# Layer 0's end in an explicit order, sort positions turned by VectorE, ties by products, and the first table tile in two halves

## The chip, the cores and the metric

The kernel runs on one core of a Trainium2 chip. A core has TensorE (matrix products, called PE in the profile, its weight loads PEld), VectorE (DVE), ScalarE (ACT), GpSimd (POOL), and SyncE (SP), which here only issues transfers. The five engines run their own instruction streams and wait for each other by semaphores. Transfers issued by SP, by ACT and by POOL run on the same 16 DMA engines. The metric is the device time of one launch in microseconds (us).

## The reference, cut to what matters

Four graph layers run one after the other on 2708 nodes of 128 features; each normalises x, applies a relu and adds its result to x. Layers 0 and 1 are the ones that the change touches:

```python
# layer 0: h = relu(layernorm(x)); A = adj, 2708 x 2708
z  = leaky_relu(lap_mul(A, h) @ W1 + b1, 0.1)       # lap_mul: d*(A @ (d*h)), d = 1/sqrt(row sums of A)
d2 = maximum(sq[:, None] + sq[None, :] - 2*(z @ z.T), 0)
S  = exp(-sqrt(d2 + 1e-10) / 2)
S  = where(rank within the row < 4, S, 0)            # only the four nearest nodes of each row stay
x  = x + lap_mul(S + A, h) @ W2 + b2
# layer 1: h = relu(layernorm(x))
XW = h @ W;  s_col = XW @ a[0, :128];  s_row = XW @ a[0, 128:]
den = exp(leaky_relu(s_row[:, None] + s_col[None, :], 0.01))
num = A @ den;  att = where(num != 0, den / num, 0)
x  = x + A @ (att @ XW)
# layer 2: h @ W_self + (A @ h / max(row sums, 1)) @ W_neigh
# layer 3: relu((A @ h) @ kernel + bias)
```

In layer 1, each column of num depends on its node only through s_col, and the leaky relu changes its slope where s_row + s_col changes its sign. If the nodes are sorted by s_row, num for any node lies between two rows of a table of running sums. The kernel builds that table instead of the dense product.

## The kernel before, in words

The 2708 nodes are cut into T = 22 tiles of 128 rows; the last, tile 21, has 20 rows. Columns are cut into six blocks of 512 (the last 148), one PSUM bank each, `acc(0)` to `acc(5)`; tiles go in six groups of four (`GROUPS`, the last one has two). Two more banks, the `ps` tiles of the pool `ps_s`, take short products in turn. The matrix comes in transposed, in row tiles ("chunks", 1354 KB each), through four buffers of the pool `big`; five tiles (17 to 21) can stay in SBUF, in buffers `res17` to `res21`.

**Order.** A scheduler behind the kernel language orders each engine's instructions by priority and readiness. `pin(ins)` ties one instruction behind the one that was written before it on its engine; `tc.issue_after` ties a block behind a given instruction. All else may move. Every engine then runs its stream in order, so that an instruction that waits holds all behind it. `pin` is used on the transfers of SP, on the first product of some groups and on some VectorE operations.

**Degree sums** (L366-405). The chunks are streamed once, TensorE adds up their rows with a matrix of ones (L373), the sums are copied out (L193, L195), turned (L395) and become d. The node features are normalised and multiplied by W1 and W2 beside this (L341, L352).

**First aggregation** (`aggregate(y1, to_z)`, products on L284). For every streamed tile, six products go into the six banks. At the end the resident tiles are added bank by bank, and `done(b)` takes each finished bank on: it becomes z, its transpose and its squared norms.

**Strips** (L510-535). For each tile TensorE makes 128 rows of the distances (L512, L520), ScalarE copies them into a strip of SBUF (L527), VectorE finds the eight largest values (MAX8, L529) and their places (FIND_INDEX8, L531). For tiles from `LATE = T - 4` on, the places are looked for later (`find_last`, L549), so that the degrees of S + A come sooner. Strips 18 and 19 have buffers of their own, all others use `big`.

**Second aggregation and the near terms** (L571-760). y2 is scaled (L577, L579), written to DRAM in two transfers (`ydr`, L583) and aggregated again. POOL gathers the near rows out of ydr, one indirect transfer for each tile and each of the four neighbours (`add_near`, L604, 88 in all, 23 buffers `gath`); VectorE adds each to xs (L610, the "near terms"). `done_l0` takes each bank on: a ScalarE copy (L650), four transposes, the addition to xs (L644), the layer norm (`layernorm_relu`, L211-221). Then come the row terms r of layer 1, for groups 0 to 3 by TensorE (`terms`) and for groups 4 and 5 by a product and a sum on VectorE (`last_terms`, L680-699), and the column terms (L708).

**Counting** (`place`, `places_of`, L808-882). The position of a node in the sorted order is a count of comparisons. For tile t VectorE compares all later nodes' r with the tile's (mask, L844), ScalarE adds up each row of the mask (L845), and TensorE adds up its columns with ones into banks 2 and 3 (L822). Within the tile itself, `own_tiles` (L722-728) makes a comparison in which a tie counts one way. After four tiles, `places_of` copies a row of counts (L858), TensorE turns it into a column by products with a single one (L862), VectorE adds the rest (L874), and POOL scatters the nodes to their places in `order_d` (L879). Between the tiles the totals are made (`total`, L913): the column sums of exp(0.01 r) A, for which 13 chunks are loaded again (L902).

**Table** (L1004-1124). The sorted list is read back and turned; `fetch(t)` (L1015) gathers 126 rows of the matrix in sorted order into `mov`; with the two running rows on top, TensorE multiplies them by `wt` (L1106), VectorE and ScalarE copy the result out (L1110, L1111), and SP stores it in the DRAM table (L1122). Then every node takes its two rows of the table (L1145), and the rest of layer 1 and layers 2 and 3 follow; the change doesn't touch them.

Of the kernel before, what the change touches and what calls it, by code (L numbers as in the profile page):

```python
# [18 lines left out]
P = 128  # L19
# [6 lines left out]
def kernel(  # L26
# [46 lines left out]
    def pin(ins):  # L73

        return tc.keep_in_program_order(ins)

# [99 lines left out]
    one_b = ones_b[:, 0:1]  # L176
# [20 lines left out]
    def acc(b):  # L197
        return ps_a.tile([P, 512], F32, name=f"acc{b}")

# [166 lines left out]
    for i in range(T):  # L366
        c = chunk(i)
        w = width(i)
        if 3 <= i < 3 + 3 * NG:
            weighted((i - 3) // 3, i % 3)  # L370
        for b, (k0, n) in enumerate(KBS):
            g = 32 * (b % 4)
            nc.tensor.matmul(  # L373
                sums[b // 4][g : g + 32, :n],
                ones[:w, :32],
                c[:w, k0 : k0 + n],
                start=(i == 0),
                stop=(i == T - 1),
            )
        if i < FIRST:  # L380
            del resident[i]
    sum_rows = lay.tile([P, 1024], F32, name="sum_rows", tag="U")
# [112 lines left out]
    LATE = T - 4  # L495
# [3 lines left out]
    def strip(t):  # L499
        if LATE <= t < LATE + 2:  # L500
            return lay.tile([P, N], F32, name=f"strip{t}", tag="UZ"[t - LATE])
# [67 lines left out]
    nc.scalar.activation(dinv2, deg2s, AF.Exp, scale=-0.5)  # L569
    y2 = lay.tile([P, T, D], F32, name="y2", tag="Y")  # L570
    ydr = dram.tile([P * T, D], F32, name="ydr")  # L571
    for i in range(2):
        resident[i] = chunk(i)
    for t0, t1 in ((0, T // 2), (T // 2, T)):
# [14 lines left out]
    for t in (T - 2, T - 1, *range(LATE, T - 2)):  # L589
# [10 lines left out]
    def add_near(t, late=False):  # L600
        w = width(t)
        for k in range(TOPK):
            g = res.tile([P, D], F32, name="gath", bufs=23)
            nc.gpsimd.indirect_dma_start(  # L604
                out=g[:w, :],
                out_offset=None,
                in_=ydr[:, :],
                in_offset=bass.IndirectOffsetOnAxis(ap=near_u[:w, t, k : k + 1], axis=0),
            )
            term = nc.vector.scalar_tensor_tensor(  # L610
                xs[:w, t, :],
                g[:w, :],
                simd[:w, t, k : k + 1],
                xs[:w, t, :],
# [3 lines left out]
            if late and k == 0:  # L618
                pin(term)
# [34 lines left out]

# [20 lines left out]
    def last_terms(g):  # L675

        t0, t1 = GROUPS[g]
        k0, n = KBS[g]
        prod = res.tile([P, 4, D], F32, name="prod")
        nc.vector.tensor_tensor(  # L680
# [4 lines left out]
        )  # L685
        e = min(t1, T - 1)
        nc.vector.tensor_reduce(r_nat[:, t0:e], prod[:, : e - t0, :], AX.X, ALU.add)
        if e < t1:
            nc.vector.tensor_reduce(
                r_nat[:TAIL, e:t1], prod[:TAIL, e - t0 : t1 - t0, :], AX.X, ALU.add  # L690
            )
        p = ps_s.tile([P, 512], F32, name="ps")
        for t in range(t0, t1):
            w = width(t)
            o = (t - t0) * P
            nc.tensor.transpose(
                p[:, o : o + w], r_nat[:w, t : t + 1].to_broadcast([w, P]), ident[:w, :w]
            )
        return nc.scalar.copy(row_all[:, k0 : k0 + n], p[:, :n])
# [13 lines left out]
    def own_tiles(g, pool):  # L713
        t0, t1 = GROUPS[g]
        for c0, c1, w in ((t0, min(t1, T - 1), P), (max(t0, T - 1), t1, TAIL)):
            n = c1 - c0
            if n <= 0:
# [3 lines left out]
            eq = pool.tile([P, 4, P], BF16, name="eq", tag="spare")[:w, :n, :w]  # L721
            pin(nc.vector.tensor_tensor(eq, rows_, mine, ALU.is_equal))  # L722
            nc.vector.tensor_tensor(
                eq, eq, tri[:w, None, :w].to_broadcast([w, n, w]), ALU.mult
            )
            o = own[:w, c0:c1, :w]
            nc.vector.tensor_tensor(o, rows_, mine, ALU.is_le)
            nc.vector.tensor_tensor(o, o, eq, ALU.subtract)


    late = {0: (15,), 1: (16,), 2: (17,), 3: (18, 19), 4: ()}

    def done_l0(g, s2):
        to_x1(g, s2)
        if g < NG - 1:
            layernorm_relu(h1, g)
            for t in late[g]:
                add_near(t, late=True)
        if 1 <= g < NG - 1:
            terms(g - 1)  # L740
        if g == NG - 1:
            last_terms(g - 1)
        if g > 2:
# [634 lines left out]
```

## Time and profile before

| what | value |
|---|---|
| three timed runs | 1194.0, 1194.6 and 1188.27 us, median 1194.0 |
| the profiled execution | 1289.18 us, of which the span from first to last instruction 1287.3 |
| PE, PEld, DVE, ACT, POOL busy | 1056.8, 499.3, 561.4, 409.7, 245.7 us |
| mean TensorE clock in that execution | 0.902 of full speed |
| DMA | 298.76 MB, 232 GB/s over the span |

The stages of that execution, from the timeline (us from the span's start):

| stage | from | to |
|---|---|---|
| degree sums | 0 | 93.5 |
| first aggregation | 93.5 | about 204 |
| strips | about 216 | 334.4 |
| second aggregation | 337.3 | 528.9 |
| end of layer 0, to the first comparison of the counting | 528.9 | 552.3 |
| counting and totals | 552.3 | 610.2 |
| table | 610.2 | 785 |
| rest of layer 1 | 785 | 960 |
| layers 2 and 3 | 960 | 1287.3 |

A line of the timeline gives the start, the duration, the engine, the line of the kernel, the operation, its output and inputs, the shape and how many there are; in brackets stands the idle time before it and what ended it. "issue" means that the engine waited for nothing that the profile shows. The clock row gives, in 40 slices of 32 us, the TensorE clock that was granted, in tenths.

### The profile page before, as it was taken

What the parts mean: (1) busy time and instruction counts of PE and PEld (TensorE: products, weight loads), DVE (VectorE), ACT (ScalarE), POOL (GpSimd) and SP (SyncE); (2) the same over time, 40 slices, a digit from 0 to 9 for tenths busy, and PEclk for the clock granted to TensorE, in tenths of its full rate; (3) what the DMA queues carried; (4) which work ended last, traced back from release to release, by engine and by line L of the source; (5) the groups of instructions that cost most, each with busy time, mean ns of one, the idle gap of its engine ahead of it and who ended that gap; (6) DMA issues with size and microseconds to landing.
All of it is one profiled execution on the core that took longest, in us unless ns stands there. A gap on an engine that the chain in (4) does not pass through costs nothing. (4 is left out here: it accounts for less than half of the span.)

```text
span 1287.3 us, 10181 instructions
## 1 busy us (share of the span) xinstructions
PE 1056.8 (82%) x3603; PEld 499.3 (39%) x3603; DVE 561.4 (44%) x1177; ACT 409.7 (32%) x636; POOL 245.7 (19%) x211
## 2 busy tenths in 40 slices
PE   4879999999763379797677771787879999999998
PEld 1324444444221134454333330333334445545444
DVE  2020026999832001783466663899970012104003
ACT  3100014544300000475567644687840012003000
POOL 4000000000277700134211103577500000000000
PEclk9989999999875579788899896698889999999999
DMA  9997800001553361256999997999949945761841
GB/s 344 422 383 276 302 3 1 1 1 43 212 202 96 94 253 50 90 233 245 274 406 395 345 348 269 423 414 419 417 184 395 326 164 181 265 245 54 306 159 43
DMA packets 38800, 298.76 MB, mean 232 GB/s; under 512 B 6735, under 2 KB 9710, under 8 KB 12290
## 3 DMA queue, kind: packets, MB, share of 16 engines
q1 hardware_dynamic: 24798, 203.76, 42.0%
q0 software_dynamic: 13952, 94.36, 19.7%
q8 instruction: 28, 0.46, 0.1%
q14 instruction: 22, 0.18, 0.0%
HBM read 265.76 MB, written 32.87 MB: 232 GB/s over the span
## 5 line engine op out<-in xcount | busy, mean ns | idle before, releaser
L284 PE MATMUL acc<-chunk,y 128*128 128x512 f32 (+1 forms) x408 | 180.3, 591 | 74.7 <-issue 58.4
L1213 PE MATMUL acc<-hi,xw 128*128 128x512 f32 (+3 forms) x264 | 124.2, 634 | 57.8 <-DVE hi L1203 57.8
L1106 PE MATMUL acc<-mov,wt 128*128 128x512 f32 (+1 forms) x264 | 115.4, 592 | 40.7 <-DMA mov<-in_adj_dram,src_u 39.2
L284 PE MATMUL acc<-chunk,h 128*128 128x512 f32 (+1 forms) x384 | 148.3, 542 | 0.0
L604 POOL DMA_INDIRECT gath<-ydr,near_u x88 | 83.8, 952 | 337.5 <-DMA ydr<-y 245.9
L284 PEld LDWEIGHTS acc<-chunk,y 128*128 128x128 f32 x408 | 79.5, 205 | 175.5 <-issue 162.0
L512 PE MATMUL acc<-zT 128*128 128x512 f32 (+2 forms) x264 | 112.7, 559 | 0.4 <-ACT strip L527 0.3
L1213 PEld LDWEIGHTS acc<-hi,xw 128*128 128x128 f32 (+1 forms) x264 | 55.7, 220 | 126.3 <-issue 66.1
L1110 DVE COPY mov<-acc 2x512 f32<-2x512 f32 x126 | 74.3, 611 | 61.1 <-PE acc L1106 60.5
L284 PEld LDWEIGHTS acc<-chunk,h 128*128 128x128 f32 x384 | 68.6, 190 | 73.2 <-issue 73.1
L1106 PEld LDWEIGHTS acc<-mov,wt 128*128 128x128 f32 x264 | 52.1, 205 | 103.8 <-issue 82.3
L527 ACT COPY strip<-acc 128x512 f32<-128x512 f32 (+2 forms) x132 | 60.7, 556 | 61.0 <-issue 35.8
L284 PE MATMUL acc<-chunk,attended 128*128 128x512 f32 x192 | 73.1, 542 | 2.5 <-DMA chunk<-in_adj_dram 2.5
L1145 POOL DMA_INDIRECT lo<-table,lo_u x22 | 58.0, 2638 | 68.6 <-issue 41.1
L1111 ACT COPY knots<-acc 128x512 f32<-128x512 f32 x88 | 50.2, 590 | 62.9 <-DVE mov L1110 56.4
L1195 ACT ACTIVATE hi<-hi,lam 128x2708 f32<-128x2708 f32 (+3 forms) x24 | 56.5, 2363 | 35.6 <-issue 26.7
L1191 DVE SCALAR_TENSOR_TENSOR hi<-lo,lam,hi 128x2708 f32<-128x2708 f32 (+3 forms) x24 | 67.1, 2801 | 1.0
L1203 DVE SCALAR_TENSOR_TENSOR hi<-row_all,inv_s,hi 128x2708 f32<-128x2708 f32 (+3 forms) x24 | 67.0, 2797 | 0.4 <-ACT hi L1196 0.4
L512 PEld LDWEIGHTS acc<-zT 128*128 128x128 f32 (+1 forms) x264 | 45.0, 185 | 51.7 <-issue 41.9
L529 DVE MAX8 top_v<-strip 128x8 f32<-128x2708 f32 (+1 forms) x22 | 64.4, 2967 | 0.4 <-ACT strip L527 0.4
L650 ACT COPY u2T<-acc 128x512 f32<-128x512 f32 (+1 forms) x6 | 3.2, 533 | 168.3 <-PE acc L284 168.2
L1196 ACT ACTIVATE hi<-hi,hb 128x2708 f32<-128x2708 f32 (+3 forms) x24 | 56.5, 2361 | 0.7
(281 smaller groups left out, 1179.5 us busy)
## 6 DMA issues: line engine op xcount, KB each, us to landing
chunk<-in_adj_dram SPq DMA_DIRECT2D x108, 1354.0 KB
table<-knots SPq DMA_DIRECT2D x20, 1354.5 KB
res<-in_adj_dram SPq DMA_DIRECT2D x9, 1354.0 KB
chunkY<-in_adj_dram SPq DMA_DIRECT2D x2, 1354.0 KB
chunkU<-in_adj_dram SPq DMA_DIRECT2D x2, 1354.0 KB
res<-in_adj_dram SPq DMA_DIRECT2D x8, 211.6 KB
ydr<-y SPq DMA_DIRECT2D x2, 704.0 KB
gath<-ydr,near_u POOLq DMA_INDIRECT x88
```

The lines of the kernel that those rows point to most:

```text
L284: nc.tensor.matmul(out[b][:, :n], y[r, i, :], chunk(i)[r, k0 : k0 + n], start=(i == 0), stop=(i == T - 2),)
L512: mm = nc.tensor.matmul(zz[b][:w, :n], zT[:, cols(t)], zT[:, k0 : k0 + n], start=True, stop=False)
L527: copied = nc.scalar.copy(s[:w, k0 : k0 + n], zz[b][:w, :n])
L529: nc.vector.max(top_v[:w, t, :], s[:w, :])
L604: nc.gpsimd.indirect_dma_start(out=g[:w, :], out_offset=None, in_=ydr[:, :], in_offset=bass.IndirectOffsetOnAxis(ap=near_u[:w, t, k : k + ...
L1106: nc.tensor.matmul(p[:, :n], wt[:, t, :], moving[t][:, k0 : k0 + n], start=True, stop=True)
L1110: nc.vector.tensor_copy(moving[t + 1][:2, k0 : k0 + n], p[:2, :n])
L1145: nc.gpsimd.indirect_dma_start(out=dst[:w, :], out_offset=None, in_=table[:, :], in_offset=bass.IndirectOffsetOnAxis(ap=idx[:w, t : t + 1] ...
L1191: nc.vector.scalar_tensor_tensor(num, lo[:w, c], kap, num, op0=ALU.mult, op1=ALU.add)
L1195: nc.scalar.activation(num, num, AF.Ln, scale=sc)
L1203: nc.vector.scalar_tensor_tensor(att[:w, c], row_all[:w, c], inv_s[:w, t : t + 1], att[:w, c], op0=ALU.max, op1=ALU.mult,)
L1213: nc.tensor.matmul(py[b][:, :n], xw[:w, t, :], att[:w, k0 : k0 + n], start=(t == T - 1), stop=(t == T - 2),)
```

## The change

It has six parts; in the diff below lines of "..." mark what is left out.

- An `Ordered` wrapper pins whatever is issued through `pe`, `dve` and `act`. `warm(p, n)` issues n pinned bf16 products of 512 columns whose result isn't used.
- Degree sums: tile 21 is taken before tile 20; three warm products follow each of the last six tiles. 16 more stand before the second aggregation and 14 before the table.
- Strips: `LATE` is T - 5; strips 17, 20 and 21 take the buffers of resident tiles 17, 18 and 19, which the second aggregation loads again (`back=5`). Four chunks instead of two are asked for ahead of the ydr writes, which are three instead of two.
- End of layer 0: the banks of groups 4 and 5 are only collected in `done_l0`; what follows is written out in order. Tile 21's four neighbours are gathered in one transfer of 4 x 32 rows, with indices and weights set in place by eight small transfers on ACT's queue, and added by one product. Group 3's row terms come from VectorE too. The transposes of groups 3 to 5 for the column terms move behind `rmax`, those column terms into `node_terms`.
- Counting: the mask takes in the tile's own columns, `own` holds only the ties on one side of the diagonal and on it, and is subtracted by a product with -1. `places_of` turns the counts by up to four VectorE transposes of 32 rows instead of copy and products. Two totals leave the loop.
- Table: tile 0 is fetched in two halves of its columns and stored in two halves.

```diff
+    class Ordered:
+        def __getattr__(self, name):
+            return lambda *a, **k: pin(getattr(self.engine, name)(*a, **k))
+    pe, dve, act = Ordered(nc.tensor), Ordered(nc.vector), Ordered(nc.scalar)
...
+    def warm(p, n):
+        for _ in range(n):
+            pin(nc.tensor.matmul(p, ident_b, ident_b[:, None, :].to_broadcast([P, 4, P]), start=True, stop=True))
...
-    for i in range(T):
+    for n_, i in enumerate([*range(T - 2), T - 1, T - 2]):
...
+        if n_ >= T - 6:
+            warm(acc(0), 3)
...
-    LATE = T - 4
+    LATE = T - 5
...
-        if LATE <= t < LATE + 2:
-            return lay.tile([P, N], F32, name=f"strip{t}", tag="UZ"[t - LATE])
+        if t in (LATE, T - 2, T - 1):
+            i = T - L0_RES + (LATE, T - 2, T - 1).index(t)
+            del resident[i]
+            return res_rows.tile([P, N + 1], F32, name=f"strip{t}", tag=f"res{i}")[:, :N]
+        if t > LATE:
+            return lay.tile([P, N], F32, name=f"strip{t}", tag="UZ"[t - LATE - 1])
...
+    warm(acc(5), 16)
...
-    for i in range(2):
+    for i in range(4):
         resident[i] = chunk(i)
-    for t0, t1 in ((0, T // 2), (T // 2, T)):
+    for t0, t1 in ((0, 9), (9, 17), (17, T)):
...
-    for t in (T - 2, T - 1, *range(LATE, T - 2)):
+    for t in range(LATE, T):
         find_last(t)
...
+    for k in range(TOPK):
+        for dst, src in ((near_p, near_u), (simd_p, simd)):
+            nc.scalar.dma_start(dst[32 * k : 32 * k + TAIL, :], src[:TAIL, T - 1, k : k + 1])
...
+    def last_near():
+        g = gathered(near_p)
+        dve.tensor_scalar(four_w, four_w, simd_p, None, op0=ALU.mult)
+        p = ps_s.tile([P, 512], F32, name="ps")
+        pe.matmul(p[:TAIL, :P], four_w[:, :TAIL], g, start=True, stop=True)
+        return p
...
-            eq = pool.tile([P, 4, P], BF16, name="eq", tag="spare")[:w, :n, :w]
-            pin(nc.vector.tensor_tensor(eq, rows_, mine, ALU.is_equal))
-            nc.vector.tensor_tensor(eq, eq, tri[:w, None, :w].to_broadcast([w, n, w]), ALU.mult)
             o = own[:w, c0:c1, :w]
-            nc.vector.tensor_tensor(o, rows_, mine, ALU.is_le)
-            nc.vector.tensor_tensor(o, o, eq, ALU.subtract)
+            pin(nc.vector.tensor_tensor(o, rows_, mine, ALU.is_equal))
+            nc.vector.tensor_tensor(o, o, tri[:w, None, :w].to_broadcast([w, n, w]), ALU.mult)
-    late = {0: (15,), 1: (16,), 2: (17,), 3: (18, 19), 4: ()}
+    late = {0: (15,), 1: (16,), 2: (17,), 3: (18,)}
...
     def done_l0(g, s2):
+        if g >= NG - 2:
+            complete.append(s2[g])
+            return
...
+    column_terms(0)
+    add_near(T - 3, dve)
+    x1(E4)
+    for t in range(*GROUPS[E4]):
+        moments(t)
+    roots(E4)
+    x1(E5)
+    normed(E4)
+    p = last_near()
+    prod = row_sums(E4 - 1)
+    natural(E4 - 1, prod)
+    as_row(E4 - 1)
+    column_terms(1)
+    column_terms(2)
+    dve.tensor_tensor(xs[:TAIL, T - 1, :], xs[:TAIL, T - 1, :], p[:TAIL, :P], ALU.add)
+    moments(T - 1)
+    add_near(T - 2, dve)
+    moments(T - 2)
+    roots(E5)
+    prod = row_sums(E4)
+    normed(E5)
+    natural(E4, prod)
+    as_row(E4)
+    natural(E5, row_sums(E5))
+    last_row = as_row(E5)
...
+        for b, (k0, n) in enumerate(KBS):
+            c0, c1 = max(a, k0), k0 + n
+            if c0 < c1:
+                count(c0, c1, ones_b, mk[:w, c0:c1], t == 0, False)
+        count(a, e, minus_b, own[:w, t, :w], False, e == N or e % 512 == 0)
...
-        mine = spare.tile([P, 512], F32, name="mine", bufs=2)
-        nc.vector.tensor_copy(mine[g : g + 1, :n], cnt[b // 4][g : g + 1, :n])
-        for t in range(t0, t1):
...
+        mine = spare.tile([P, 4, 32], F32, name="mine", bufs=2)
+        rows_ = cnt[b // 4][g : g + 32, :].rearrange("p (t f) -> p t f", f=P)
+        for r in range(0, P, 32):
+            m = sum(r < width(t) for t in range(t0, t1))
+            nc.vector.transpose(mine[r : r + 32, :m, :], rows_[:, :m, r : r + 32])
...
-        if 1 <= t <= len(here) + 4 or t in (15, 16, 18, 20):
+        if 1 <= t <= len(here) + 4 or t in (16, 19):
             total(done)
...
+        for c in (slice(0, HALF), slice(HALF, N)) if t == 0 else (slice(0, N),):
+            nc.gpsimd.indirect_dma_start(
+                out=m[2:, c],
...
+                element_offset=c.start,
...
     weights(0)
+    warm(acc(5), 14)
...
-            nc.sync.dma_start(table[t * P + s0 : (t + 1) * P, :], o[s0:, :])
+            for c in (slice(0, HALF), slice(HALF, N + 1)) if t == 0 else (slice(0, N + 1),):
+                nc.sync.dma_start(table[t * P + s0 : (t + 1) * P, c], o[s0:, c])
```

## The prediction

> **What bounds the kernel now.** I read the page first (shares, clock row), then 25-us windows, then the timeline by engine where a slice looks odd, then the waits of the counting stage.
>
> ```profile
> span 1287.3 us, 10181 instructions
> ...
> PE 1056.8 (82%) x3603; PEld 499.3 (39%) x3603; DVE 561.4 (44%) x1177; ACT 409.7 (32%) x636; POOL 245.7 (19%) x211
> ...
> PEclk9989999999875579788899896698889999999999
> ```
>
> TensorE carries the kernel, but its clock sags in slices 12 to 15. The windows (us, busy time with count for PE, PEld, DVE, ACT, POOL, then clock, DMA share, GB/s) show why:
>
> ```profile
> 350.00:375.00 25.00, 20.28 (x52) 9.04 (x51) 9.19 (x31) 0.00 (x0) 18.90 (x21) 0.94 0.66 244
> 375.00:400.00 25.00, 7.88 (x9) 2.54 (x9) 6.89 (x21) 0.00 (x0) 18.90 (x21) 0.50 0.36 107
> 400.00:425.00 25.00, 7.89 (x9) 2.58 (x9) 6.05 (x18) 0.00 (x0) 18.91 (x21) 0.50 0.35 108
> 425.00:450.00 25.00, 8.89 (x9) 2.69 (x10) 0.00 (x0) 0.00 (x0) 17.80 (x19) 0.50 0.34 104
> ```
>
> TensorE does nine matmuls in 25 us and waits for nothing visible, while POOL issues gathers at an undisturbed pace. This execution took 1289.2 us (span 1287.3 and 1.9 around it), the timed runs 1188.3 to 1194.6, median 1194.0: 95.2 less. The same 132 products take 99 us in the undisturbed aggregation (1182.5 to 1281.3). Begun at 337.3, with 1.8 us of half clock, they would end at 438.4, not 528.9: 90.5 us. I therefore take the crawl to belong to the profiled execution; that is an inference.
>
> Without the crawl, who ends layer 0? The timeline has the pieces (start, duration, then idle before and its releaser):
>
> ```profile
> 79.07 1.90 PE L373 MATMUL ps<-res,ones 128*32 128x512 f32 x12 [0.62 <-DMA res<-in_adj_dram]
> ...
> 84.85 5.38 PE L373 MATMUL ps<-res,ones 128*32 128x512 f32 x24 [3.13 <-DMA res<-in_adj_dram]
> ...
> 326.22 2.67 ACT L527 COPY strip<-acc 20x512 f32<-20x512 f32 x6 [2.76 <-issue]
> ...
> 331.40 2.96 DVE L529 MAX8 top_v<-strip 20x8 f32<-20x2708 f32 x1
> ...
> 344.20 1.03 POOL L604 DMA_INDIRECT gath<-ydr,near_u  x1 [245.88 <-DMA ydr<-y]
> ...
> 447.34 0.95 POOL L604 DMA_INDIRECT gath<-ydr,near_u  x1 [0.30 <-issue]
> ...
> 552.28 1.56 DVE L844 TENSOR_SCALAR mask<-row_all,r_nat 128x2580 bf16<-128x2580 f32 x1 [0.78 <-ACT row_all L699]
> ...
> 619.71 7.16 PE L1106 MATMUL acc<-mov,wt 128*128 128x512 f32 x12 [6.53 <-DMA mov<-in_adj_dram,src_u]
> ```
>
> From 344.20 to 447.34 there are 83 gathers, 103.1/82 = 1.26 us each (the last five waited for buffers). All 88 end their issue at 344.2 + 88 x 1.26 = 455.1; a gather is used 3.0 us after its issue starts (the 60th starts near 418.5, its term runs at 421.2), so the last term is near 457. From the last term (547.7) to the first mask (552.28) takes 4.6, so the mask begins near 461. By TensorE: 438.4 plus the profile's 23.4 us from last product to mask gives 461.8. Counting back, 1194.0 less the 1.9 and the 735.0 from mask to end gives 457. So **POOL's gathers and the engines' tail end layer 0 within a few us of each other**, both well behind the last product.
>
> [...] after 3.13 us of idleness 24 sums take 5.38 us where 12 took 1.90, and at 93.5 starts are 0.85 apart, 0.43 after 98.8. [...] the 3.0 above includes 0.95 of issue.
>
> **The change part by part.**
>
> *1. Degree sums.* The 20-row tile 21 goes ahead of tile 20, and three bf16 matmuls follow each of the last six tiles. Behind the last transfer there remain 12 sums at full clock, 1.9, not 24 at half, 5.38: -3.5. The small transfer now goes first: 212 KB at 423 GB/s is 0.5, and if it spreads badly 0.8: +0.65. The next aggregation starts warm: its first 5.3 us of half-speed starts (93.5 to 98.8) take half, -2.7. The final three warm matmuls, [...] lie in the 0.88 us in which TensorE waits for sum_rows. **-5.5** (0 if the clock still drops, to -6.5).
>
> *2. Strips.* From 216.8 VectorE runs without a gap to 334.4: 22 MAX8 and 18 FIND_INDEX8 at 2.9. LATE one lower moves one FIND behind the sums: -2.9, but the last strip is complete only at 328.9, so MAX8 ends at 331.9: **-2.5** (0 to -2.9). The moved search is five times 3.0 instead of four, in front of the near terms only; POOL runs ahead by 23 buffers (29 us). Chunks 2 and 3 are issued by SP ahead of the ydr writes; their buffers come free near 317, so SP isn't held. In exchange three resident tiles are reloaded: 3 x 3.3 = 9.9 us of DMA inside the aggregation; even as a full TensorE stall it ends at 434.1 + 9.9 = 444, before the gathers. The 16 warm matmuls [...] lie between 328.9, when their bank is copied out, and 334.8[...]. They and the warm start end the products 1.8 earlier, which waits for gathers.
>
> *3. Layer 0's end.* Tile 21's four gathers become one with a 0.2-us matmul: 3 x 1.26 = **-3.8** (0 to -7, if the engine order alone was binding). Eight small DMAs on ACT's queue, 0.8 each by SP's three y copies in 2.44 us, 6.5 in all, run near 353; ACT's next work is the first bank, near 420 without the crawl. The pinned VectorE order waits for tile 19's terms (443), with x1, moments and row sums, about 5 us, queued behind; tile 20's terms come at 449.7, so this fits with a us to spare. After the last term prod (0.69) comes before the reciprocal, in a 0.5-us wait: +0.2; ydr in three pieces, -0.3. hT's three transposes and their ACT copies (0.59, 0.59, 0.28) move into the counting stage; they hold the two ps buffers before the totals for about 1 us, covered by VectorE's masks.
>
> *4. Counting.* The waits of 575 to 612 (engine, waited for: us, times, longest):
>
> ```profile
> PE acc L862 <- DVE mine L858: 5.8, 3, 3.5
> DVE to_u L874 <- PE acc L862: 3.4, 3, 1.9
> ```
>
> VectorE loses five copies of 0.68 and one of 0.30 (3.7) and gains 24 transposes of 32 rows by up to 128 columns. The trace has none; nearest are 128 columns from PSUM at 0.29 and 1x512 at 0.68. [...] so I take 0.28: +6.7. Bounds: half of that, +3.4, and twice the 512-column copy, 1.36 each, +32.6. Ties: is_le and subtract go, group 1 moves in: 6.1 to 5.3, -0.8. Masks widen by 128 columns, 0.07 x 22 = +1.5, two extra short ones +0.4. Sum +4.1 of VectorE work; half of it falls in the first 25 us, where VectorE is full: +2. The round trip through TensorE, 3.4, goes. **-1.5** (-5 to +6 short of the dear transpose). Behind a transpose the next masks queue, as behind the copy before. Twelve column-term matmuls (about 0.15 each) move in too, off the path: VectorE doesn't wait for them before tile 16. Two totals leave the loop; the trace already has seven after the last count (598.9 to 610.2), with the turn of the sorted list pinned behind them, so I count nothing; a further total there would cost 1.1 to 1.9.
>
> *5. Table start.* Half a fetch lands first: its data came from about 614 to 619.7, and the first 57% would be there near 617.2; 14 warm matmuls [...] keep the clock, so the first twelve take about 5 instead of 7.2. The store begins near 621.5, not 628; but DMA share is 1.0 from there to 750, so only the mixing with fetches helps: DMA moves 211 to 249 GB/s at 620-630 and over 400 later; 6.5 us x 150 GB/s is 1 MB, 2.4 us. The extra fetch issue is +1.05 on POOL, hidden by queued data. The first tile's store in two costs SP one more issue of 0.33, where SP waits for copies. **-2.0** (0 to -4).
>
> Sum: -5.5 - 2.5 - 3.8 - 1.5 - 2.0 = -15.3. On the profiled execution 1289.2 - 15.3 = 1273.9, if its crawl kept its length; on the median **1178.7, so 1179**.
>
> **Rivals.** *A, the clock stays low and the tail isn't gather-bound.* Parts 1 and 3 give nothing, 4 and 5 half: 1194 - 2.5 - 1.8 = 1189.7. For it: the tie at 461; against: 81.8 to 84.85 is the only long gap there. *B, the halves don't lead*: the first product waits for the whole fetch, and counting, fed by an unbroken 36-us stream of chunks (561 to 597), gives nothing. 1194 - 11.8 = 1182.2. *C, slower: VectorE's transposes.* With price p, and VectorE then the bound of the whole stage, part 4 is 24p - 3.7 - 0.8 + 1.9 - 3.4 = 24p - 6.0. At 1.36 that is +26.6, and 1194 - 13.8 + 26.6 = 1206.8. It decides from 24p - 6.0 = 13.8, at 0.83 us each. Against it: no PSUM operation of 128 columns here takes over 0.35.
>
> **How the numbers follow.** Forecast 0.58, B 0.17, A 0.13, C 0.12. Half a per cent (6 us) is what a measurement tells from no change. Faster 0.75, same 0.13, slower 0.12. The best ends give about 1169; forecast alone 1170 to 1187. To leave out 2 in 10 the range goes to A and stops short of C: 1167 to 1196.
>
> **What the profile would show.** Right: L373's last tile near 1.9; one FIND fewer before the last MAX8; 85 gathers; transposes near 0.28; first L1106 twelve near 5 us, two early stores. Wrong: transposes above 0.6, TensorE waiting for chunks behind the reloads, VectorE idle in the pinned order after its last gather has landed.

## The result and the profile after

| | median | lowest to highest | runs |
|---|---|---|---|
| kernel before | 1192.45 us | 1188.27 to 1196.36 | 20 |
| changed kernel | 1187.68 us | 1184.36 to 1193.61 | 20 |

The ratio is 0.9962, with a 95% interval from 0.9946 to 0.9978: 4.8 us faster by the medians, about a third of the 15.3 forecast. A repetition of the changed kernel gave 0.9972 (0.9952 to 0.9992), 2.8 us by the medians. Ratios are not quotients of the medians; where the two differ much, both are given.

On some of the chips used, every execution of every kernel, timed ones too, shows the crawl of TensorE that the prediction describes and takes about 70 to 90 us more, while on others none does, so figures are compared within one chip's runs unless the text says otherwise. The profile of before that the prediction read has the crawl; the profile after has not.

The page of the changed kernel:

```profile
span 1183.2 us, 10230 instructions
...
PE 1029.7 (87%) x3613; PEld 488.3 (41%) x3613; DVE 561.0 (47%) x1190; ACT 409.0 (35%) x636; POOL 243.6 (21%) x209
...
PEclk9999999999998995989989857899999999999999
```

The row of 5 to 7 in slices 12 to 15 of the clock is gone. Because of that a plain comparison of the two profiles misleads: the crawl stood between them, and so did its after-effects. The timeline of the changed kernel, with the lines that answer to those of the prediction:

```profile
86.51 1.90 PE L396 MATMUL ps<-res,ones 128*32 128x512 f32 x12
...
324.76 2.97 DVE L559 MAX8 top_v<-strip 20x8 f32<-20x2708 f32 x1 [0.29 <-ACT strip L557]
...
330.65 27.53 PE L306 MATMUL acc<-chunk,y 128*128 128x512 f32 x72 [2.26 <-DVE y L610]
361.38 21.43 PE L306 MATMUL acc<-chunk,y 128*128 128x512 f32 x48 [3.20 <-DMA chunk<-in_adj_dram]
386.23 32.04 PE L306 MATMUL acc<-chunk,y 128*128 128x512 f32 x84 [3.41 <-DMA chunk<-in_adj_dram]
...
443.69 0.94 POOL L647 DMA_INDIRECT gath<-ydr,near_u  x1 [0.30 <-DVE xs L699]
446.75 0.87 PE L84 MATMUL ps<-ident,u2T 128*128 128x128 f32 x6 [0.27 <-ACT u2T L84]
...
454.56 1.48 DVE L84 SCALAR_TENSOR_TENSOR xs<-gath,simd,xs 128x128 f32<-128x128 f32 x4
...
460.97 1.63 DVE L982 TENSOR_SCALAR mask<-row_all,r_nat 128x2708 bf16<-128x2708 f32 x1 [1.46 <-ACT row_all L84]
...
521.70 4.71 PE L1245 MATMUL acc<-mov,wt 128*128 128x512 f32 x12
530.94 6.48 PE L1245 MATMUL acc<-mov,wt 128*128 128x512 f32 x12 [3.64 <-DMA mov<-in_adj_dram,src_u]
```

What to see: the degree sums of the last tile run warm (1.90 us). The second aggregation stops twice for a chunk, 3.20 and 3.41 us, after reloads went out on the same queue. The last gather is issued at 443.69, but its term is added only at 454.56, where VectorE's written order puts it: the gathers don't set the end. The first table products start early and at full clock (granted 1.00 from 521.7 to 526.4 us; 0.67 in the profile of before, 619.7 to 626.9), and the second tile then waits 3.64 us for its rows.

The kernel before without the crawl is seen in one of the runs below, which differs from it only in the table stage (`table_only`). Its timeline up to there:

```profile
332.00 79.61 PE L294 MATMUL acc<-chunk,y 128*128 128x512 f32 x204 [9.60 <-DVE y L589]
...
448.25 0.89 POOL L614 DMA_INDIRECT gath<-ydr,near_u  x1 [0.30 <-issue]
448.88 0.67 PE L272 MATMUL ps<-ident,u2T 128*128 128x128 f32 x2
449.59 0.35 DVE L654 SCALAR_TENSOR_TENSOR xs<-ps,dinv,xs 128x128 f32<-128x128 f32 x1 [1.97 <-PE ps L272]
...
453.30 0.69 DVE L690 TENSOR_TENSOR prod<-h,wrow 128x512 f32<-128x512 f32 x1 [1.72 <-ACT h L231]
454.03 0.69 DVE L697 TENSOR_REDUCE r_nat<-prod 128x4 f32<-128x512 f32 x1
454.63 1.76 DVE L620 SCALAR_TENSOR_TENSOR xs<-gath,simd,xs 128x128 f32<-128x128 f32 x5
...
462.41 1.56 DVE L854 TENSOR_SCALAR mask<-row_all,r_nat 128x2580 bf16<-128x2580 f32 x1 [0.78 <-ACT row_all L709]
...
476.32 1.20 POOL L889 DMA_INDIRECT order_d<-pay,to_u  x1 [27.18 <-DVE to_u L884]
...
508.74 0.90 POOL L889 DMA_INDIRECT order_d<-pay,to_u  x1 [0.30 <-issue]
```

Here 204 products run without a gap. The last gather is issued at 448.25, and the trace has its data landed at 450.45. VectorE reaches the last terms only at 454.63. Before them, in its stream, stand the additions of the last bank, which wait for TensorE's transposes (449.59), and then the row terms of group 4, which wait for ScalarE (453.30). TensorE makes the transposes of the last bank at 448.88, 9.9 us after its last product at 439.0: in its stream stand, ahead of them, transposes of group 3, row terms and column terms, three of which wait for ScalarE. In the changed kernel the transposes come at 446.75, 1.1 us after the last product at 445.65. From each profile the length of each stage, in us:

| kernel, one profiled execution each, no crawl | first to second aggregation | products of the second | last product to first mask | mask to first table fetch | fetch to row gathers (L1145; L1285 after) |
|---|---|---|---|---|---|
| table_only (stands for before) | 242.8 | 107.0 | 23.4 | 52.8 | 173.1 |
| changed kernel | 238.6 | 115.0 | 15.3 | 53.5 | 166.1 |
| changed kernel, again | 240.3 | 114.9 | 15.3 | 53.5 | 168.8 |
| reload_only | 244.3 | 115.9 | 23.3 | 53.3 | 171.7 |
| order_count | 243.7 | 108.5 | 15.4 | 53.5 | 168.9 |
| old_strips2 | 241.1 | 108.5 | 16.9 | 52.2 | 168.9 |
| late_reload2 | 238.6 | 111.5 | 15.3 | 53.4 | 169.6 |

Two columns in the middle carry the case: layer 0's end won 8.1 us, and the products ahead of it lost 8.0.

### The profile page after: what moved, and what is told of

It is laid out like the page before. It is cut to its first block, busy times and chain, and to the rows that moved or that the text cites. A ratio compares the mean times of both kernels' runs of the same rounds, so it can differ in the third digit from the quotient of the medians.

```text
span 1183.2 us, 10230 instructions
## 1 busy us (share of the span) xinstructions
PE 1029.7 (87%) x3613; PEld 488.3 (41%) x3613; DVE 561.0 (47%) x1190; ACT 409.0 (35%) x636; POOL 243.6 (21%) x209
## 5 line engine op out<-in xcount | busy, mean ns | idle before, releaser
L1353 PE MATMUL acc<-hi,xw 128*128 128x512 f32 (+3 forms) x264 | 119.0, 610 | 61.2 <-DVE hi L1343 61.2
L306 PE MATMUL acc<-chunk,y 128*128 128x512 f32 (+1 forms) x408 | 158.5, 550 | 10.7 <-DMA chunk<-in_adj_dram 6.6
L1245 PE MATMUL acc<-mov,wt 128*128 128x512 f32 (+1 forms) x264 | 115.0, 589 | 28.4 <-DMA mov<-in_adj_dram,src_u 28.0
L647 POOL DMA_INDIRECT gath<-ydr,near_u x84 | 80.8, 961 | 265.7 <-DMA ydr<-y 240.4
L306 PEld LDWEIGHTS acc<-chunk,y 128*128 128x128 f32 x408 | 74.5, 193 | 94.9 <-issue 88.4
L1353 PEld LDWEIGHTS acc<-hi,xw 128*128 128x128 f32 (+1 forms) x264 | 53.5, 211 | 126.7 <-DVE hi L1343 64.3
L1245 PEld LDWEIGHTS acc<-mov,wt 128*128 128x128 f32 x264 | 51.9, 204 | 91.1 <-issue 71.9
L1285 POOL DMA_INDIRECT lo<-table,lo_u x22 | 56.1, 2549 | 66.9 <-DMA table<-knots 33.9
L1109 ACT ACTIVATE sg<-row_all,c_nat 128x2708 bf16<-128x2708 f32 (+1 forms) x22 | 56.3, 2559 | 0.1
```

What stands on the lines that cost most here:

```text
L306: nc.tensor.matmul(out[b][:, :n], y[r, i, :], chunk(i)[r, k0 : k0 + n], start=(i == 0), stop=(i == T - 2),)
L647: nc.gpsimd.indirect_dma_start(out=g[: idx.shape[0], :], out_offset=None, in_=ydr[:, :], in_offset=bass.IndirectOffsetOnAxis(ap=idx, axis=0),)
L1245: nc.tensor.matmul(p[:, :n], wt[:, t, :], moving[t][:, k0 : k0 + n], start=True, stop=True)
L1353: nc.tensor.matmul(py[b][:, :n], xw[:w, t, :], att[:w, k0 : k0 + n], start=(t == T - 1), stop=(t == T - 2),)
```

## The experiments

**The reloads alone.** The kernel before, three resident tiles dropped and read again:

```diff
+    for i in range(T - L0_RES, T - L0_RES + 3):
+        del resident[i]
-    aggregate(y2, done_l0, ..., kept=4)
+    aggregate(y2, done_l0, ..., kept=4, back=5)
```

> The kernel before with three resident tiles dropped ahead of the second aggregation and read again from its fifth chunk on, nothing else; no work is left out. Theory 'reloads cancel': the products take 115 us instead of 107 and the end moves with them, 7 to 9 us slower, ratio 1.006 to 1.0075. Rival 'covered', as the prediction had it: 9.9 us of DMA disappear in the stage, within 0.1 % of the kernel before. If TensorE crawls in the second aggregation, both say no difference.

Measured: 1201.06 us, ratio 1.0061 (1.0044 to 1.0079): 9.05 us slower by the medians, 7.3 by the ratio. The products, from its timeline:

```profile
335.67 11.35 PE L284 MATMUL acc<-chunk,y 128*128 128x512 f32 x24 [8.13 <-DVE y L579]
347.27 18.41 PE L284 MATMUL acc<-chunk,y 128*128 128x512 f32 x48 [0.25 <-DMA chunk<-in_adj_dram]
367.68 9.32 PE L284 MATMUL acc<-chunk,y 128*128 128x512 f32 x24 [2.00 <-DMA chunk<-in_adj_dram]
379.76 11.02 PE L284 MATMUL acc<-chunk,y 128*128 128x512 f32 x24 [2.75 <-DMA chunk<-in_adj_dram]
392.14 32.04 PE L284 MATMUL acc<-chunk,y 128*128 128x512 f32 x84 [1.36 <-DMA chunk<-in_adj_dram]
```

The one run of 204 breaks into five, with waits for chunks; 8.9 us more of products, and the time to the mask behind them stays 23.3. So the reloads cost nearly the whole 9.9 us of DMA that the prediction gave them, and it lies on the path. Why nothing hides them is seen in the windows of the kernel without reloads (us, busy time with count for PE, PEld, DVE, ACT, POOL, then clock, DMA share, GB/s; `table_only`):

```profile
352.00:372.00 20.00, 20.00 (x55) 9.58 (x54) 5.95 (x19) 0.00 (x0) 15.13 (x17) 1.00 1.01 400
372.00:392.00 20.00, 20.00 (x54) 9.40 (x53) 5.66 (x16) 0.00 (x0) 15.13 (x17) 1.00 1.01 393
```

TensorE is never idle, yet the DMA engines are full too: the chunks arrive just as fast as they are used up. One more transfer delays the next chunk, as reload_only shows.

**The written order without the reloads.** `old_strips2` is the changed kernel with the last strips where they were (two prefetched chunks, `back` not given); `order_count` takes away the first and fifth part as well:

```diff
-    LATE = T - 5
+    LATE = T - 4
-        if t in (LATE, T - 2, T - 1):
-            i = T - L0_RES + (LATE, T - 2, T - 1).index(t)
-            del resident[i]
-            return res_rows.tile(...)
...
-    aggregate(y2, done_l0, ..., kept=4, back=5)
+    aggregate(y2, done_l0, ..., kept=4)
```

> The changed kernel with the last strips where they lay before (from T - 4 on, two of them in U and Z, none on a resident tile), so that nothing is read again in the second aggregation; nothing is left out. Theory 'reloads cancel': the products take 107 us instead of 115, the end of layer 0 keeps its 15.3 us from last product to first mask, the second aggregation starts some 2 us later than in the changed kernel: 9 to 11 us less than the kernel before, ratio 0.9905 to 0.9925, faster than the changed kernel (0.997). Rival 'gathers': with the products done 8 us earlier the gathers are the last to end, and the time from last product to first mask grows by 5 us or more: ratio 0.995 to 0.997.

> The changed kernel without its first, second and fifth part: tile 20 of the degree sums in its old place, strips where they were, table not in halves; what stays are the written order at layer 0's end with the merged gathers and the counting. Nothing is left out. Theory 'reloads cancel': last product to first mask 15.3 us instead of 23.4, products 107 us: 7 to 9 us faster, ratio 0.9925 to 0.994. Rival 'gather-bound', as the prediction had it: 3.8 us from the order and 1.5 from the counting at most, ratio 0.9955 or above.

Measured: old_strips2 1184.04 us, 0.9932 (0.9903 to 0.9961); order_count 1184.61 us, 0.9933 (0.9905 to 0.9961); before 1192.01. The order and the counting gain 7.4 us without the reloads, where the whole change gained 4.8 and 2.8 in its own sets of runs. order_count keeps the 16 warm products and the ydr writes in three pieces, and it has the merged gathers together with the written order; these were not run apart. What old_strips2 has more, the parts 1 and 5, adds 0.6 us (by resampling the runs, anything from 4.4 gained to 5.5 lost). The rival of old_strips2 has a small share: its gathers are issued 2.9 us later, and VectorE now waits for three of them.

```profile
451.18 0.35 DVE L84 SCALAR_TENSOR_TENSOR xs<-gath,simd,xs 128x128 f32<-128x128 f32 x1 [0.32 <-DMA gath<-ydr,near_u]
452.18 0.35 DVE L84 SCALAR_TENSOR_TENSOR xs<-gath,simd,xs 128x128 f32<-128x128 f32 x1 [0.66 <-DMA gath<-ydr,near_u]
453.19 0.35 DVE L84 SCALAR_TENSOR_TENSOR xs<-gath,simd,xs 128x128 f32<-128x128 f32 x1 [0.66 <-DMA gath<-ydr,near_u]
```

These waits, 1.64 us together, make up the difference in the time from last product to mask, 16.9 us instead of 15.3. That the two versions beat the changed kernel where nothing crawls is likely and not settled: they were not run beside it on such a chip, and across the sets of runs the quotient of the ratios (each by the mean of both ratios of the changed kernel) is 0.9965 with an interval from 0.9935 to 1.001 for old_strips2, and 0.9966 (0.9937 to 0.9997) for order_count, worked out by resampling the runs.

**The reloads later.** One number in the changed kernel, `back=5` to `back=11`, beside the changed kernel in one set of runs.

> The changed kernel once more, unedited, as the yardstick for the run that follows. If TensorE crawls in the second aggregation here too (one product per 2.8 us for some 90 us), both theories say the crawl does not depend on the change: about 0.992 of the kernel before (-9 to -11 us of some 1284, because the products then end after the gathers in both kernels). If it does not crawl, both say 1187.7 within 2 us, and a ratio of 0.996.

> The changed kernel with the three resident tiles read again after the eleventh instead of the fifth chunk of the second aggregation; nothing is left out. Theory 'reloads': the early reloads hold up the chunks, and every microsecond of that is on the path because layer 0's end hangs on the last product: 6 to 10 us less than the unedited changed kernel in the same session (1178 to 1182 without the crawl, some 1268 with it), and the waits for chunks of 3.2 and 3.4 us are gone. Rival 'order': the written order at layer 0's end costs what is missing, and the reloads cost nothing: within 2 us of the unedited changed kernel.

Measured: 1190.04 and 1186.35 us, before 1192.86; ratios to before 0.9972 and 0.9924 (0.9897 to 0.9951). Against each other 0.9969, with an interval from 0.9933 to 0.9991 by resampling: 3.7 us less, half of what was expected. The timeline of the later reloads:

```profile
386.07 9.32 PE L306 MATMUL acc<-chunk,y 128*128 128x512 f32 x24 [0.58 <-DMA chunk<-in_adj_dram]
397.92 10.88 PE L306 MATMUL acc<-chunk,y 128*128 128x512 f32 x24 [2.53 <-DMA chunk<-in_adj_dram]
410.01 4.78 PE L306 MATMUL acc<-chunk,y 128*128 128x512 f32 x12 [1.20 <-DMA chunk<-in_adj_dram]
```

The products run without a stop up to 385 us, and smaller waits follow the later reloads: 4.3 us in all instead of 6.6, products 111.5 us, between 107 and 115. My expectation that all waits would go was wrong.

**Single parts.** Each is the kernel before with one part of the change; the edits are those of the change's diff (for `degree_only` the order of the last two tiles and `warm(acc(0), 3)`; for `count_only` masks, ties and transposes; for `table_only` both halves and the 14 warm products).

> The kernel before with the degree sums of the change alone (tile 21 ahead of tile 20, three warm matmuls after each of the last six). By the trace after, the first aggregation begins 1.4 us earlier and skips 2.6 us of half clock: 4.0 us faster than before, ratio 0.9966. Rival: a later stage takes it back (near terms or transfers set the end of layer 0): ratio 0.999 to 1.0.

> The kernel before with the counting part alone (masks from the diagonal tile on, ties by a product of -1, positions turned by VectorE); nothing is left out. Theory 'as seen': mask to first fetch shrinks by the 5.9 us that the two profiles show (59.4 to 53.5 us), ratio 0.9950 to 0.9957. Rival 'as predicted': only 1.5 us come from this part and the rest from the order ahead of it, ratio 0.9985 to 0.9990.

> The kernel before with the table part alone (first tile fetched and stored in two halves, 14 products to warm TensorE); nothing is left out. Theory 'as seen': first fetch to the first gather of the attended rows shrinks by the 7.7 us of the two profiles (173.8 to 166.1 us), ratio 0.9935 to 0.9945. Rival 'as predicted': 2 us, ratio 0.998 to 0.9988; and if the products of the knots are held up by the warm-up at half clock, up to 1 us slower.

Measured: degree_only 1280.48 us against 1283.91, 0.9975 (0.9954 to 0.9997), on a chip with the crawl, whose stage lies behind this one. count_only 1190.64, 0.9979 (0.9955 to 1.0003). table_only 1193.98, 1.0002 (0.9983 to 1.0021). The expectations "as seen" for the last two took the stage differences of the two profiles for the parts' own, and fell: in profiles without the crawl the counting takes 52.8 us in the old form (table_only) and 52.6 in the new (count_only). With the crawl before it, the same stage took 58.6 to 59.4 us in the kernel before, and 55.5 to 60.3 in variants with the new counting; the difference of 5.9 us came with the crawl. That the counting alone gained its 2.2 us isn't clear of noise. Its profile shows 1.4 of them ahead of the counting: from last product to mask 22.0 us instead of 23.4. In the old form three comparisons for `own` of 0.65 to 0.67 us (L737 in table_only, at 450.18, 450.87 and 456.87) lie in that stretch of VectorE's stream, and in the new form they are gone.

Nor do the halves shorten the stage of the table: from the first fetch to the row gathers it took 173.1 us with them (table_only) and 172.7 without (count_only) on one chip. One difference stays open. Without the crawl the stage took 166.1 to 169.6 us in the five executions with the new end of layer 0, order_count without halves among them, and 171.7 to 173.1 in the three with the old end; with the crawl the two kinds overlap, 165.2 to 173.8 and 167.1 to 173.8. The windows of the changed kernel say why a better start isn't kept:

```profile
535.00:575.00 40.00, 33.24 (x96) 16.52 (x95) 27.01 (x63) 29.27 (x39) 6.29 (x6) 0.92 1.01 391
575.00:615.00 40.00, 33.28 (x98) 16.86 (x97) 25.99 (x58) 26.77 (x37) 5.24 (x5) 0.91 1.01 395
```

The DMA engines are full from the second tile on. The first twelve products end 11.9 us after the fetch is issued (521.70 + 4.71 - 514.52) instead of 15.2 (619.71 + 7.16 - 611.71); the second twelve end 22.9 us after it in the changed kernel, and 20.6 in the kernel before (627.59 + 4.71 - 611.71).

**The crawl.** The kernel before again, and the changed kernel with the later reloads and with the old strips, on a chip with the crawl:

> The kernel before, profiled once more. If the crawl of 90 us in the second aggregation belongs to profiling, its length changes or it is gone, and the first comparison of the counting starts between 455 and 462 us. If it belongs to the kernel, TensorE again makes nine matmuls in 25 us from 375 to 450, and the span is near 1287.

> The changed kernel with the three resident tiles asked for from step 11 of the second aggregation on, not from step 5. Theory 'reloads': their 9.9 us of transfers in the middle starve TensorE (waits of 3.2 and 3.4 us for chunks in the profile after) and the end of layer 0 is products plus tail, so products end and counting start 5 to 9 us earlier and the time falls from 1187.7 to 1179 to 1183. Rival 'order': the pinned order of VectorE makes the tail slow by itself and covers the waits; time within 2 us of 1187.7.

> The changed kernel with the strips as before: LATE at T-4, strips 20 and 21 in the streaming buffers, two chunks asked for ahead, nothing reloaded. Theory 'reloads': the loss of 5 to 9 us in the second aggregation goes, the gain of 2.5 us in the strips goes too; 1181 to 1185. Rival 'order': only the strips' gain is lost, 1190.

Measured: before 1283.57 us in that run and 1283.91 (1275.06 to 1291.28) over 26; late_reload 1267.96, 0.9861 (0.9826 to 0.9896); old_strips 1274.32, 0.9900 (0.9862 to 0.9938). The times expected were for executions without a crawl, so these two told nothing of their own question; they were run again as late_reload2 and old_strips2. What they did tell is that timed runs crawl as well. Two further sets of runs were meant to compare the changed kernel and the old strips side by side, and to try one reload instead of three (strip 20 on tile 17's buffer, three prefetched chunks). Both fell on chips with the crawl:

> The changed kernel unedited, as the yardstick for the two runs that follow: 0.9955 to 0.9985 of the kernel before, products 115 us and 15.3 us from the last product to the first mask in both theories.

> As old_strips2: the changed kernel with the last strips where they lay before and nothing read again. Theory 'reloads cancel': 3 to 6 us below the changed kernel of the same session (about 0.9965 of it). Rival: the earlier start of the second aggregation (2.5 us later here) and the gathers, which now end last, give it all back: within 1.5 us of the changed kernel.

> As old_strips3, but strip 20 takes the buffer of resident tile 17, which alone is read again, and three chunks instead of two are asked for ahead of the ydr writes. Theory 'reloads cancel': the products take a third of the extra time, 109.5 to 111.5 us, the start comes at most 1 us earlier, so 1 to 3 us above old_strips3. Rival, a threshold: one tile of 3.3 us fits into the slack of the transfers, products within 1 us of old_strips3 and the time within 1 us or below.

> The changed kernel unedited, as the yardstick for the two that follow. 0.9955 to 0.9985 of the kernel before if TensorE does not crawl in the second aggregation, about 0.98 if it does.

> The changed kernel with the last strips where they lay before and nothing read again; nothing is left out. Theory 'reloads cancel': 3 to 6 us below the changed kernel of the same session where TensorE does not crawl (about 0.9965 of it); where it crawls, the transfers have 80 us of idle products to hide in and the earlier gathers decide: 6 to 10 us above it. Rival: no difference within 1.5 us.

Measured, by chip: changed kernel 1256.60 (0.9796, 0.9761 to 0.9831), old_strips3 1265.59 (0.9865, 0.9828 to 0.9902), one_reload 1264.02 (0.9884, 0.983 to 0.9939); then changed kernel 1263.48 (0.9849, 0.9814 to 0.9885), old_strips4 1270.29 (0.9888, 0.9857 to 0.9920). There the changed kernel is the faster one, by 9 and 7 us, and is worth 1.5 to 2 % against the kernel before. An explanation that fits, but was not tested: the crawl ends with the gathers, which begin 6.1 and 2.9 us sooner in these profiles of the changed kernel, and at nine products in 25 us a reload has time to land. One reload was to show whether the cost grows by tiles; with the crawl over it, it can't, and that stays open.

One more edit takes 45 gathers away, and with them three quarters of the near terms of tiles 0 to 14:

```diff
-        for k in range(TOPK):
+        for k in range(1 if t < 15 else TOPK):
             g = gathered(near_u[:, t, k : k + 1])
```

> The changed kernel with one gather instead of four for each of the tiles 0 to 14, 45 gathers fewer; three quarters of these tiles' near terms are left out. Without the crawl: theory 'the last product decides' says within 0.2 % of the changed kernel (a little less where 45 times 66 KB of DMA are missed); rival 'gather-bound', as the prediction had it, says 3 us or more faster. With the crawl: theory 'it belongs to the gathers' says that it ends some 45 x 1.26 = 57 us sooner, with the last gather; rival 'it has a length of its own' says 80 to 90 us as before.

Measured: 1208.70 us against 1263.48 of the changed kernel on the same chip, 54.8 less, where 57 were expected. Windows of the changed kernel there (`after_fourth`):

```profile
375.00:400.00 25.00, 7.63 (x10) 2.59 (x9) 6.53 (x20) 0.00 (x0) 18.91 (x21) 0.50 0.33 109
400.00:425.00 25.00, 8.22 (x10) 2.58 (x9) 5.00 (x15) 0.00 (x0) 18.93 (x20) 0.50 0.46 163
```

and of the kernel with 45 gathers fewer:

```profile
375.00:400.00 25.00, 13.32 (x21) 5.30 (x21) 0.00 (x0) 0.00 (x0) 8.70 (x10) 0.58 0.49 176
400.00:425.00 25.00, 23.32 (x62) 10.99 (x61) 0.00 (x0) 0.00 (x0) 0.00 (x0) 1.00 0.97 402
```

The crawl starts at about 369 in both, some 30 us after the first gather, and ends a few microseconds after the row of gathers does: 390.8 against a last issue at 386.4. So on that chip its length hangs on the gathers; what in them stops TensorE, and why not on other chips, stays open.

## Why the prediction was wrong

**The step that failed is in part 2: "even as a full TensorE stall it ends at 434.1 + 9.9 = 444, before the gathers".** What was wrong is what the 444 was held against. The prediction had itself worked out two ends for the kernel before, 461 by the gathers and 461.8 by TensorE's last product and the 23.4 us behind it, and then used only the first. Compared with the gathers' end, a product that ends at 444 is early; but it has 15.3 to 23.4 us of work behind it. So the reloads, forecast at nothing, cost their time in full: reload_only measured +9.05 us (+7.3 by the ratio), and the products of the changed kernel take 8.0 us more. The prediction's own sign of being wrong, "TensorE waiting for chunks behind the reloads", is in the profile after with 3.20 and 3.41 us. That the products do end at 445.6, near the 444, is in part luck: with the 5.5 us of part 1 taken off as well, the same sum gives 438.5, and it allowed 109.2 us of products, where 115.0 were needed.

**A second term was far too large: part 1, -5.5.** The degree sums do what was said, 1.90 us for the last tile, but the 5.38 us that they replace is not the rule in the kernel before. These are the last sums in the old order, in count_only and in order_count:

```profile
84.13 5.38 PE L374 MATMUL ps<-res,ones 128*32 128x512 f32 x24 [2.32 <-DMA res<-in_adj_dram]
...
83.79 3.73 PE L396 MATMUL ps<-res,ones 128*32 128x512 f32 x24 [1.97 <-DMA res<-in_adj_dram]
```

Of six profiled executions with the old sums, two waited 3.13 and 2.32 us for the last chunks and took 5.38 us; four waited 1.25 to 1.97 us and took 3.73 to 3.76. So the -3.5 rested on one profile. The first aggregation starts at 89.2 to 93.5 us with the old sums and at 91.1 to 93.6 with the new, not sooner. What is left is its warmer start (granted clock 1.00 from 92 to 100 us in the profile after, 0.50 from 94 to 98 in that of before): from it to the second aggregation 242.8 to 244.3 us with the old sums, 241.1 to 242.8 with the new ones and the old strips. The clearest measurement is old_strips2 against order_count: 0.6 us for parts 1 and 5 together, where 7.5 were forecast. The -3.4 of degree_only (0.9954 to 0.9997, a gain of 0.4 to 5.9 us) is too broad to decide.

**The strips of part 2, -2.5:** with them that stretch is 238.6 to 240.3 us, so they gain about what was forecast, 0.8 to 4.2 us; the reloads buy it at 8.

**Part 3, -3.8, had its mechanism wrong and its size too small.** It counted three gathers at 1.26 us off a gather-bound end. In the kernel before, VectorE comes to the last gathered rows 4.2 us after the last of them has landed (454.63 against 450.45); in the changed one the last landing isn't in the trace, but with the 2.5 to 6.5 us from issue to landing that are, it lies 4 to 8 us ahead of its term (454.56). The 3.0 us that the prediction took for a gather were read under the crawl, at a DMA share of 0.35; in table_only, at 1.01, the median is 5.7. What the part does is shorten the work between the last product and the mask, 23.4 to 15.3 us: -8.1, near the -7 that stood as its other end, "if the engine order alone was binding". The traces put most of it down to TensorE's stream, where the transposes of the last bank come 1.1 us after the last product instead of 9.9; 1.4 us belong to the counting. What the written order does and what the merged gathers do was not run apart. order_count confirms it with -7.4 for this part and the counting together. That the pinned order "fits with a us to spare" held.

**Part 4, -1.5:** the transposes cost 0.31 us each (x20, 6.2 us in all) where the author's estimate was 0.28, so rival C, which needed 0.83, never came near. The copies and the round trip went, but the stage is 53.5 us instead of 52.8. POOL's 22 scatters take most of it, 32.4 us from first to last before and 31.7 after, and the first of them comes 15.9 us after the first mask instead of 13.9. count_only measured -2.2, with an interval that includes nothing. The prediction's readings of waits inside this stage were of a stage that was longer on the chip with the crawl.

**Part 5, -2.0:** nothing (1.0002). The halves lead as said, the first product comes 7.2 us after the fetch instead of 8.0 and at a clock of 1.00. The prediction saw the DMA share of 1.0 behind it and still credited 6.5 us at 150 GB/s; the second tile gives the lead back.

**The crawl** was said to "belong to the profiled execution". It goes with the chip, or with the set of runs, for each chip was used in one set only: on one of them 26 runs of the kernel before lay from 1275 to 1291. Whether the first profile was taken on another chip than the three times beside it, its records do not tell. The subtraction that followed from it, 90.5 us, was nearly right: without the crawl the products were to take 438.4 - 337.3 = 101.1 us (its terms, 99 and 1.8, give 100.8), and took 107.0. The crawl depends on the number of gathers, 54.8 us less with 45 fewer (few_gathers); by what mechanism was not shown.

By size, rival A, 1189.7, came closest. It was right in that the tail isn't gather-bound, and in that part 1 gives next to nothing; it was wrong in why: TensorE's clock is up (1.00 from 84 to 100 us in the profile after), part 3 with the counting gave about twice its forecast, and the reloads took that away. In terms of the stages against table_only: -8.1 for the end, +8.0 for the reloads, -2.5 to -4.2 ahead of them, +0.7 for the counting; sum -2 to -4, measured -4.8 and -2.8 by the medians. The agreement is rough. The sum leaves out the start of the first aggregation, 1.9 and 2.9 us later in the two profiles of the changed kernel, and the stage of the table, 4.3 and 7.0 us shorter in them, and it compares single executions.

## What to carry to other kernels

Where two chains end within a microsecond of each other, a cost must be held against both of them, each with all the work that follows its last step: here a transfer that was to end before the gathers lay on the other chain in full. In a stage in which TensorE and the DMA engines were both full (table_only: 20.00 us busy of 20.00, DMA share 1.01), more transfers were not hidden: three of them, 9.9 us by the prediction's estimate, made the products 8.9 us longer. A lead won at the start of such a stage can be given back inside, as the second tile of the table did. And stages of two profiles may be compared only if both ran under the same conditions; the difference of a stage that the edit doesn't touch tells whether they did.

## What the runs showed of the hardware that was not expected

- On three of the five chips of the experiments, TensorE issues one product per 2.8 us during a long row of indirect gathers from POOL (at 1.25 us each), with no wait that the profile shows; on the two others, with the same kernels and gathers, it has no such stretch. It starts 24 to 32 us into the row and ends some 5 to 12 us after its last issue. On those chips counting, with its 22 indirect scatters, also takes 55.5 to 60.4 us instead of 52.2 to 53.5.
- TensorE's clock fell to 0.50 in the last degree sums after a wait of 2.32 us (count_only, 86 to 88 us), and stayed at 1.00 after one of 1.97 us (order_count, 84 to 88 us). The length of a gap alone doesn't decide it: ahead of the first aggregation a gap of 1.76 us went with 0.50 in order_count (90 to 96 us) and in the profile of before (94 to 98 us), and one of 1.80 us with 1.00 in the profile after (92 to 100 us). The prediction had read the fall after 3.13 us of idleness; in count_only the shorter gap was enough.
- A gather of POOL lands 2.2 to 7.6 us after its issue in table_only, 5.7 us in the median of those whose landing the trace has.
- 14 warm products of 512 bf16 columns in front of the table took 5.27 us, 0.38 each, and most of them ran at the lower clock that they were to end (0.50 from 516 to 520 us); behind the last strip 16 took 3.61, 0.23 each, at 1.00.
- VectorE's transpose of 32 x 128 f32 from PSUM takes 0.31 us, of 32 x 32 0.21 us.
